# Second attention: the scores by head on 32 rows instead of against masked queries, and the turning of rows as a step of its own

## The chip, the cores and the metric

The kernel runs on one core of one Trainium2 chip. The metric is the device time of one execution in microseconds. A core has five engines that run their own instruction streams: TensorE (PE, matmuls, with weight loads that overlap them), VectorE (DVE), ScalarE (ACT), GpSimd (POOL) and SyncE (SP, which here issues transfers). They wait for one another through semaphores. Matmuls write PSUM, eight banks of 512 f32 columns on 128 partitions; DVE and ACT read results from there.

## The reference

The input is x, 8 blocks of 512 tokens by 256. Two layers follow, each of the form x + attention(layernorm(x)) + mixture of experts(layernorm(x)). The first attention has 16 heads with a causal softmax. Both mixtures have 8 experts, of which each token uses 2. The change touches the second attention only, a gated linear recurrence over 8 heads of 32:

```python
def step(M, inp):
    q_t, k_t, v_t, f_t, g_t, o_t = inp
    M = M * f_t[..., None, None] + g_t[..., None, None] * scale * (k_t[..., :, None] * v_t[..., None, :])
    y_t = jnp.einsum('bhd,bhde->bhe', q_t, M) * o_t[..., None]
    return (M, y_t)
_, yT = jax.lax.scan(step, M0, (qT, kT, vT, fT, gT, oT))
```

q and k are projected from an RMS-normed x and rotated (rope); f, g and o are sigmoids of three more projections; y goes through Wout and a bias is added.

## The kernel before

The recurrence is computed in chunks. A block of S = 512 tokens is NT = 4 chunks of P = 128. Within a chunk, y is a causally masked product: scores (k against q, per head) times exp of the summed logs of f between the two tokens, times v. Between chunks a state m per head is carried: y gets q, weighted by the decay, against m, and m is decayed and gets k, weighted, against v.

The work on a block has two parts. `prep1` prepares: four steps `s_proj` (matmuls pa and pb at L1282 on PE, rope in four instructions from L1297 on DVE, v copied by ACT at L1307), then `s_gates` (the sigmoids by an Exp and a Ln, L1319 and L1323, on ACT, and products on DVE) and `s_decays` (cumulated sums dec on PE, L1343 to L1352, ew and tot by Exp on ACT, and lfx, a copy on ACT). `main1` computes, in steps per chunk c:

- `s_scores(c)`: ACT makes u, eight copies of a triangle of ones, each scaled by a head's log f (L1402). PE turns q and k of the chunk (four transposes qkT, L1406) and ACT copies them to SBUF (qkTs, L1408). Then for each half hf of four heads: PE adds a large negative mask (bf16, L1412) and the summed logs gt·u (L1419) into a bank d; ACT takes exp (de, L1423); DVE spreads the turned queries of four heads over a block-diagonal tile (qb, L1426), so that one full product of 128 rows by 512 columns gives the scores of four heads (a, L1433); DVE multiplies (am, L1434).
- `s_chunk(c)`: for c > 0, the weighted queries qw are turned (qwT, L1449) and copied by ACT (qwTs, L1451). y is made per half from the state (L1454) and four value products, each on a column group of 32 (L1458), and is copied by ACT (yTs, L1466). For c < 3, pm (L1474) is the chunk's addition to the state, taken over by DVE with tm and m (L1488, L1489). po = y·Wout (L1496) is added to x by DVE (L1499).

The chunk step lags one behind the scores: scores 0, scores 1, chunk 0, scores 2, chunk 1, and so on. `interleave` mixes the steps of `main1` of a block with the `prep1` steps of the next block in proportion; the last block of a part has no successor and runs without. After each step `move` deals some steps of other work, in a number worked out from `n_steps`. A scheduler then orders the instructions of each engine by its own estimate of when they can run, so the order on an engine is not just the order of the code. Each engine runs its stream in that order: an instruction that waits holds up all behind it.

`attention1` runs twice. Part a takes blocks 0 to 3 (about 1040 to 1303 us) and deals out the norm, logits, choice of experts (rt_both L315, rank L322, rt_tot L325) and the 128 scatters of rows to the second mixture (L437, on POOL). The experts of the second mixture follow (1303 to 1828 us), among them `prep1` of block 4. Part b takes blocks 4 to 7 (1828 to 1997 us) and deals out the additions of the experts' results (L476, DVE).

PSUM pools of a part: mm (two banks: pa, pb, po and dealt work), tr (two: qkT, qwT), da (two: d and a), y (one), sm (one: dec and pm).

Of the kernel before, what the change touches and what calls it, by code (L numbers as in the profile page):

```python
# [8 lines left out]
F32 = mybir.dt.float32  # L9
# [8 lines left out]
P = 128  # L18
# [66 lines left out]
def tile_two_layers(  # L85
# [1165 lines left out]
    def prep1(b, ap, ps_mm, ps_sm, held1, places=None):  # L1251

        wide = {"tag": "mm", "n": S} if places else {"tag": "sm", "n": 256}
# [86 lines left out]
        def s_decays():  # L1340
            flat = lf.rearrange("p t h -> p (t h)")
            ps = ps_sm.tile([P, wide["n"]], F32, tag=wide["tag"], name=f"dec{b}")
# [27 lines left out]
    def attention1(blocks, part, also, done, held1):  # L1370
        with tc.tile_pool(name=f"a1{part}", bufs=2) as ap, tc.tile_pool(
            name=f"a1mm{part}", bufs=2, space=PSUM
        ) as ps_mm, tc.tile_pool(name=f"a1tr{part}", bufs=2, space=PSUM) as ps_tr, tc.tile_pool(
            name=f"a1da{part}", bufs=2, space=PSUM
        ) as ps_da, tc.tile_pool(name=f"a1y{part}", bufs=1, space=PSUM) as ps_y, tc.tile_pool(
            name=f"a1sm{part}", bufs=1, space=PSUM
        ) as ps_sm:
            wout = second["wout"]
            moves = deque(also(ap, ps_mm))
            n_steps = len(blocks) * (3 * NT + 2)  # L1380
# [8 lines left out]
            def main1(b):  # L1389
# [8 lines left out]
                def s_scores(c):  # L1398

                    u = ap.tile([P, H1, P], F32, tag="u", name=f"u{b}_{c}")  # L1400
                    for h in range(H1):
                        nc.scalar.activation(u[:, h, :], inc, AF.Copy, scale=lf[:, c, h : h + 1])  # L1402
# [6 lines left out]
                    am = ap.tile([P, 2, 4, P], F32, tag="am", name=f"am{b}_{c}")  # L1409
                    for hf in range(2):  # L1410
                        pd = ps_da.tile([P, 4, P], F32, tag="da", name=f"d{b}_{c}_{hf}")
                        nc.tensor.matmul(  # L1412
                            pd,
                            ident_h,
                            mask_gt.unsqueeze(1).to_broadcast([P, 4, P]),
# [3 lines left out]
                        nc.tensor.matmul(  # L1419
                            pd, gt, u[:, 4 * hf : 4 * hf + 4, :], start=False, stop=True  # L1420
                        )
                        de = ap.tile([P, 4, P], F32, tag="de", name=f"de{b}_{c}_{hf}")
                        nc.scalar.activation(de, pd, AF.Exp)  # L1423

                        qb = ap.tile([P, 4, P], F32, tag="qb", name=f"qb{b}_{c}_{hf}")
                        nc.vector.tensor_tensor(  # L1426
                            qb,
                            qkT[:, hf, :].unsqueeze(1).to_broadcast([P, 4, P]),
# [8 lines left out]
                def s_chunk(c):  # L1437
# [3 lines left out]
                    if c:  # L1441
                        pt = ps_tr.tile([P, 4, P], F32, tag="tr", name=f"qwT{b}_{c}")
# [248 lines left out]
```

## Time and profile before

| | us |
|---|---|
| time, median of 3 runs | 2000.53 (1999.66 to 2000.71) |
| the profiled execution | 1999.08 |
| its span (2.1 us lie around it) | 1997.0 |
| mean granted clock of TensorE | 0.96 |
| busy: PE | 1817.4 |
| busy: DVE | 829.4 |
| busy: ACT | 794.5 |
| part a, PE busy of 1040 to 1303 us | 199.9 |
| part b, PE busy of 1828 to 1997 us | 155.7 |

The page of the profile gives busy times per engine, the span in 40 slices, the chain of work that ended last, and groups of instructions. A group's line gives the source line, the engine, the operation, output <- inputs, the shape and the number of instructions; behind the first bar the busy time and the mean in ns of one; behind the second bar the idle time of the engine just before these instructions, and what ended it. Matmuls are pipelined: the length shown of one is more than what it costs, so costs are read from start to start in the timeline. f32 products appear as two instructions each.

### The profile page before, as it was taken

Reading aid. Unit: us, or ns where it says so; the run is one execution under the profiler, and the core shown is the slowest. Engines: PE = TensorE matmul, PEld = TensorE weight load, DVE = VectorE, ACT = ScalarE, POOL = GpSimd, SP = SyncE. Lnnn points to the kernel's source line nnn. Section 1 sums busy time; section 2 is a strip of 40 time slices with the busy share of each in tenths; the row PEclk is TensorE's granted clock in tenths of the full one; section 3 lists DMA queues with packets and bytes.
Section 4 is the critical chain, followed back from the end, with each engine's and each line's share of the span. In section 5 each row is a group of like instructions: output and inputs, shape, how many; then the busy total and the mean of one; then the engine's idle time right before and its main releaser. Section 6 shows DMA issues by size and latency. Waiting matters only on the chain. (4 is left out here: it accounts for less than half of the span.)

```text
span 1997.0 us, 28227 instructions
## 1 busy us (share of the span) xinstructions
PE 1817.4 (91%) x10680; PEld 1241.0 (62%) x10680; DVE 829.4 (42%) x1886; ACT 794.5 (40%) x1452; POOL 401.8 (20%) x457
## 2 busy tenths in 40 slices
PE   5988989999999999998778479999999999999998
PEld 3435655666666665664344235578888889887555
DVE  5453234344344444344676346641111111114865
ACT  2333434444434444444335044533333233325455
POOL 2015531221211221211130661011111111011000
PEclk9999999999999999999789679999999999999899
DMA  8723321754534443332330330076676867581500
GB/s 249 180 93 102 97 65 41 224 191 134 173 122 133 136 172 125 114 120 72 120 111 32 117 106 14 1 258 224 226 256 212 311 216 263 212 301 66 172 11 22
DMA packets 163687, 289.17 MB, mean 145 GB/s; under 512 B 63952, under 2 KB 134624, under 8 KB 152928
## 3 DMA queue, kind: packets, MB, share of 16 engines
q1 hardware_dynamic: 148432, 248.77, 38.3%
q0 software_dynamic: 13088, 36.07, 4.9%
q10 hardware_dynamic: 2032, 2.54, 0.4%
q8 instruction: 84, 1.38, 0.3%
q14 instruction: 51, 0.42, 0.1%
HBM read 206.78 MB, written 67.94 MB: 138 GB/s over the span
## 5 line engine op out<-in xcount | busy, mean ns | idle before, releaser
L659 PE MATMUL gup<-xgT,ew 128*128 128x256 f32 (+1 forms) x2080 | 386.0, 338 | 4.5 <-issue 2.7
L692 PE MATMUL gdn<-ew,hgT 128*128 128x256 f32 x1640 | 376.6, 383 | 0.0
L659 PEld LDWEIGHTS gup<-xgT,ew 128*128 128x128 f32 x2080 | 331.7, 192 | 47.4 <-issue 10.3
L692 PEld LDWEIGHTS gdn<-ew,hgT 128*128 128x128 f32 x1640 | 307.8, 191 | 50.8 <-issue 11.5
L966 DVE TENSOR_REDUCE mx<-m 128x4 f32<-128x2048 f32 (+3 forms) x128 | 190.2, 1486 | 269.5 <-PE m L965 248.7
L991 ACT ACTIVATE pt<-s 128x2048 f32<-128x2048 f32 (+3 forms) x128 | 158.4, 1237 | 199.6 <-PE s L987 186.6
L719 POOL DMA_INDIRECT zd<-yo,row x144 | 140.6, 976 | 466.3 <-DVE yo L710 403.4
L993 POOL TENSOR_SCALAR_AFFINE_SELECT pt<-pt 128x512 f32<-128x512 f32 x128 | 83.8, 655 | 668.2 <-ACT pt L991 666.9
L670 ACT ACTIVATE hgT<-gup,ew 128x256 f32<-128x256 f32 (+1 forms) x376 | 133.9, 423 | 208.4 <-issue 123.6
L710 DVE SCALAR_TENSOR_TENSOR yo<-ew,way,yo 128x256 f32<-128x256 f32 x72 | 31.7, 481 | 300.3 <-ACT yo L708 300.3
L961 PE MATMUL m<-k,q 32*128 32x512 f32 (+3 forms) x1024 | 123.3, 489 | 23.6 <-ACT pt L991 18.4
L987 PE MATMUL s<-qsh,k 32*128 32x512 f32 (+3 forms) x1024 | 113.1, 499 | 31.5 <-DVE mx L966 30.5
L437 POOL DMA_INDIRECT xd<-xr,pos x128 | 126.2, 986 | 55.8 <-issue 44.5
L991 ACT ACT_TABLE_LOAD x52 | 66.7, 1283 | 121.8 <-PE s L987 121.0
L961 PEld LDWEIGHTS m<-k,q 32*128 32x128 f32 x1024 | 48.3, 186 | 80.8 <-ACT pt L991 52.4
L987 PEld LDWEIGHTS s<-qsh,k 32*128 32x128 f32 x1024 | 42.9, 191 | 88.7 <-DVE mx L966 67.9
L1011 PE MATMUL av<-pt,vaug 128*32 128x256 f32 (+3 forms) x1024 | 89.1, 453 | 4.6 <-POOL pt L993 4.5
L1020 DVE STREAM_TRANSPOSE ou<-av 128x512 f32<-128x512 f32 x32 | 22.9, 716 | 146.7 <-PE av L1011 132.5
L708 ACT ACTIVATE yo<-gdn,way 128x256 f32<-128x256 f32 x72 | 30.2, 473 | 125.8 <-PE gdn L692 125.7
L1419 PE MATMUL d<-u,cs 128*128 128x512 f32 x128 | 71.5, 642 | 4.2 <-ACT u L1402 3.9
L1433 PE MATMUL a<-qb,qkTs 128*128 128x512 f32 x128 | 70.0, 629 | 3.8 <-DVE qb L1426 1.9
L1402 ACT ACTIVATE u<-cs,lf 128x128 f32<-128x128 f32 x224 | 72.2, 393 | 0.0
(254 smaller groups left out, 2361.4 us busy)
## 6 DMA issues: line engine op xcount, KB each, us to landing
ew<-in_dram SPq DMA_DIRECT2D x47, 2180.0 KB
ew<-in_dram SPq DMA_DIRECT2D x36, 1024.0 KB
xd<-zero SPq DMA_DIRECT2D x12, 1572.0 KB
z<-zd SPq DMA_DIRECT2D x32, 512.0 KB
xnT<-in_dram SPq DMA_DIRECT2D x22, 512.0 KB
xg<-xd SPq DMA_DIRECT2D x36, 262.0 KB
xg<-xd SPq DMA_DIRECT2D x144, 64.0 KB
xn_d<-l_xn SPq DMA_DIRECT2D x16, 512.0 KB
```

Of the source, the lines that this page charges most:

```text
L437: i = nc.gpsimd.indirect_dma_start(out=self.xd, out_offset=bass.IndirectOffsetOnAxis(ap=self.pos[k][:, at : at + 1], axis=0), in_=held[b][ ...
L659: nc.tensor.matmul(ps[:, j, at : at + m], wu[u][:, k, f * P : (f + 1) * P], x, start=(k == 0), stop=(k == KD - 1),)
L670: nc.scalar.activation(ht[:, f, at : at + m], ps[:, j, at : at + m], AF.Gelu, bias=w[u][2][:, f : f + 1],)
L692: nc.tensor.matmul(ps[:, t, :], ht[:, f, t * P : (t + 1) * P], wd[:, f, :], start=(f == 0), stop=(f == nf - 1),)
L719: d = nc.gpsimd.indirect_dma_start(out=self.r.zd, out_offset=bass.IndirectOffsetOnAxis(ap=row[:, s : s + 1], axis=0), in_=y[:, s, :], in_o ...
L961: nc.tensor.matmul(ps[:, h, :w], q[r, j * P : w], k[r, :w], start=True, stop=False)
L966: last["dve"] = nc.vector.tensor_reduce(mxs[n % 2][:, j, :, HD0], ps[:, :, :w], AX.X, ALU.max)
L987: nc.tensor.matmul(ps[:, h, :w], k[r, i * P : (i + 1) * P], q[r, i * P :], start=True, stop=True)
L991: nc.scalar.activation(e, ps[:, :, :w], AF.Exp, scale=0.25)
L993: last["pool"] = nc.gpsimd.affine_select(out=e[:, :, :P], in_=e[:, :, :P], pattern=[[0, 4], [1, P]], base=0, channel_multiplier=-1, compar ...
L1011: nc.tensor.matmul(ps[32 * h : 32 * h + 32, i * P :], vaugs[b % 2][:, i, c : c + 32], e[:, h, :], start=(i == 0), stop=(i == NT - 1),)
L1402: nc.scalar.activation(u[:, h, :], inc, AF.Copy, scale=lf[:, c, h : h + 1])
```

## The change

The turning of rows and u become a step `s_turn(c)`. `s_scores(c)` takes one tile of four banks. In each bank r lie the scores of heads r and r + 4 in the first two quarters, from products of 32 rows by 128 columns on row group r, and the summed logs of the same heads in the last two. All scores are written first; then mask and gt·u for each bank; then one exp and one product am over all eight heads. qb and the full product a are gone. The order of y is state, values of both halves, state. The chunk step lags two behind the scores, and `n_steps` counts four steps per chunk. Pools: tr has one bank instead of two, da one tile of four banks instead of two of one, sm is gone: pm lies in the second half of qwT's tile, dec in mm.

The core of the diff (left out: `prep1` loses its parameter `ps_sm` and takes dec's bank from mm, and its call during the experts follows):

```diff
@@ -1370,14 +1368,12 @@
     def attention1(blocks, part, also, done, held1):
         with tc.tile_pool(name=f"a1{part}", bufs=2) as ap, tc.tile_pool(
             name=f"a1mm{part}", bufs=2, space=PSUM
-        ) as ps_mm, tc.tile_pool(name=f"a1tr{part}", bufs=2, space=PSUM) as ps_tr, tc.tile_pool(
-            name=f"a1da{part}", bufs=2, space=PSUM
-        ) as ps_da, tc.tile_pool(name=f"a1y{part}", bufs=1, space=PSUM) as ps_y, tc.tile_pool(
-            name=f"a1sm{part}", bufs=1, space=PSUM
-        ) as ps_sm:
+        ) as ps_mm, tc.tile_pool(name=f"a1tr{part}", bufs=1, space=PSUM) as ps_tr, tc.tile_pool(
+            name=f"a1da{part}", bufs=1, space=PSUM
+        ) as ps_da, tc.tile_pool(name=f"a1y{part}", bufs=1, space=PSUM) as ps_y:
             wout = second["wout"]
             moves = deque(also(ap, ps_mm))
-            n_steps = len(blocks) * (3 * NT + 2)
+            n_steps = len(blocks) * (4 * NT + 2)
             left = [n_steps]
 
             def move():
@@ -1395,51 +1391,57 @@
                 def per_head(a):
                     return a.unsqueeze(2).to_broadcast([P, H1, HD1])
 
-                def s_scores(c):
-
-                    u = ap.tile([P, H1, P], F32, tag="u", name=f"u{b}_{c}")
+                turns = {}
+
+                def s_turn(c):
+
+
+                    u = ap.tile([P, 4, 2, P], F32, tag="u", name=f"u{b}_{c}")
                     for h in range(H1):
-                        nc.scalar.activation(u[:, h, :], inc, AF.Copy, scale=lf[:, c, h : h + 1])
+                        nc.scalar.activation(
+                            u[:, h % 4, h // 4, :], inc, AF.Copy, scale=lf[:, c, h : h + 1]
+                        )
                     pt = ps_tr.tile([P, 4, P], F32, tag="tr", name=f"qkT{b}_{c}")
                     flat = qk[c].rearrange("p h d -> p (h d)")
                     for i in range(4):
                         nc.tensor.transpose(pt[:, i, :], flat[:, i * P : (i + 1) * P], ident)
                     qkT = ap.tile([P, 4, P], F32, tag="qkT", name=f"qkTs{b}_{c}")
                     nc.scalar.copy(qkT, pt)
-                    am = ap.tile([P, 2, 4, P], F32, tag="am", name=f"am{b}_{c}")
+                    turns[c] = qkT, u
+
+                def s_scores(c):
+                    qkT, u = turns.pop(c)
+                    ps = ps_da.tile([P, 4, 4, P], F32, tag="da", name=f"da{b}_{c}")
                     for hf in range(2):
-                        pd = ps_da.tile([P, 4, P], F32, tag="da", name=f"d{b}_{c}_{hf}")
+                        for r in range(4):
+                            rows = slice(32 * r, 32 * r + 32)
+                            nc.tensor.matmul(
+                                ps[:, r, hf, :],
+                                qkT[rows, 2 + hf, :],
+                                qkT[rows, hf, :],
+                                start=True,
+                                stop=True,
+                            )
+                    for r in range(4):
                         nc.tensor.matmul(
-                            pd,
+                            ps[:, r, 2:, :],
                             ident_h,
-                            mask_gt.unsqueeze(1).to_broadcast([P, 4, P]),
+                            mask_gt.unsqueeze(1).to_broadcast([P, 2, P]),
                             start=True,
                             stop=False,
                         )
-                        nc.tensor.matmul(
-                            pd, gt, u[:, 4 * hf : 4 * hf + 4, :], start=False, stop=True
-                        )
-                        de = ap.tile([P, 4, P], F32, tag="de", name=f"de{b}_{c}_{hf}")
-                        nc.scalar.activation(de, pd, AF.Exp)
-
-                        qb = ap.tile([P, 4, P], F32, tag="qb", name=f"qb{b}_{c}_{hf}")
-                        nc.vector.tensor_tensor(
-                            qb,
-                            qkT[:, hf, :].unsqueeze(1).to_broadcast([P, 4, P]),
-                            blk.unsqueeze(2).to_broadcast([P, 4, P]),
-                            ALU.mult,
-                        )
-                        pa = ps_da.tile([P, 4, P], F32, tag="da", name=f"a{b}_{c}_{hf}")
-                        nc.tensor.matmul(pa, qkT[:, 2 + hf, :], qb, start=True, stop=True)
-                        nc.vector.tensor_mul(am[:, hf], pa, de)
+                        nc.tensor.matmul(ps[:, r, 2:, :], gt, u[:, r], start=False, stop=True)
+                    de = ap.tile([P, 4, 2, P], F32, tag="de", name=f"de{b}_{c}")
+                    nc.scalar.activation(de, ps[:, :, 2:, :], AF.Exp)
+                    am = ap.tile([P, 4, 2, P], F32, tag="am", name=f"am{b}_{c}")
+                    nc.vector.tensor_mul(am, ps[:, :, :2, :], de)
                     got[c] = am
 
                 def s_chunk(c):
                     am = got.pop(c)
 
                     py = ps_y.tile([P, 2, P], F32, tag="y", name=f"y{b}_{c}")
-                    if c:
-                        pt = ps_tr.tile([P, 4, P], F32, tag="tr", name=f"qwT{b}_{c}")
+                    pt = ps_tr.tile([P, 4, P], F32, tag="tr", name=f"qwT{b}_{c}")
                     if c:
 
                         qw = ap.tile([P, H1, HD1], F32, tag="qw", name=f"qw{b}_{c}")
@@ -1449,19 +1451,23 @@
                             nc.tensor.transpose(pt[:, hf, :], flat[:, hf * P : (hf + 1) * P], ident)
                         qwT = ap.tile([P, 2, P], F32, tag="qwT", name=f"qwTs{b}_{c}")
                         nc.scalar.copy(qwT, pt[:, :2, :])
-                    for hf in range(2):
+                    def of_state(hf):
                         if c:
                             nc.tensor.matmul(
-                                py[:, hf, :], m[:, hf, :], qwT[:, hf, :], start=True, stop=False
+                                py[:, hf, :], m[:, hf, :], qwT[:, hf, :], start=hf == 0, stop=hf == 1
                             )
+
+                    of_state(0)
+                    for hf in range(2):
                         for h in range(4):
                             nc.tensor.matmul(
                                 py[32 * h : 32 * h + 32, hf, :],
                                 v[:, c, 4 * hf + h, :],
-                                am[:, hf, h, :],
-                                start=(c == 0),
-                                stop=True,
+                                am[:, h, hf, :],
+                                start=(c == 0 or hf == 1),
+                                stop=(c == 0 or hf == 0),
                             )
+                    of_state(1)
                     yT = ap.tile([P, KD, P], F32, tag="yT", name=f"yTs{b}_{c}")
                     nc.scalar.copy(yT, py)
 
@@ -1469,7 +1475,7 @@
 
                         kw = ap.tile([P, H1, HD1], F32, tag="kw", name=f"kw{b}_{c}")
                         nc.vector.tensor_tensor(kw, qk[c][:, H1:], per_head(ew[:, 1, c]), ALU.mult)
-                        pm = ps_sm.tile([P, 256], F32, tag="sm", name=f"pm{b}_{c}")
+                        pm = pt[:, 2:, :].rearrange("p i t -> p (i t)")
                         for hf in range(2):
                             nc.tensor.matmul(
                                 pm[:, hf * P : (hf + 1) * P],
@@ -1500,14 +1506,16 @@
 
                 steps = []
                 for c in range(NT):
+                    steps.append(lambda c=c: s_turn(c))
+                    if c > 1:
+                        steps.append(lambda c=c: s_chunk(c - 2))
                     steps.append(lambda c=c: s_scores(c))
-                    if c:
-                        steps.append(lambda c=c: s_chunk(c - 1))
+                steps.append(lambda: s_chunk(NT - 2))
                 steps.append(lambda: s_chunk(NT - 1))
                 return steps
 
             def prep(b):
-                return prep1(b, ap, ps_mm, ps_sm, held1)
+                return prep1(b, ap, ps_mm, held1)
 
             if blocks[0] not in held1:
                 interleave(prep(blocks[0]), [], move)
```

More of the change, by code (lines that the diff above doesn't have):

```diff
@@ L1246, in tile_two_layers, with prep1 @@
         move(len(moves))
-    def prep1(b, ap, ps_mm, ps_sm, held1, places=None):
-        wide = {"tag": "mm", "n": S} if places else {"tag": "sm", "n": 256}
+    def prep1(b, ap, ps_mm, held1, places=None):
         wcat = second["wcat"]
@@ L1341, in s_decays @@
             flat = lf.rearrange("p t h -> p (t h)")
-            ps = ps_sm.tile([P, wide["n"]], F32, tag=wide["tag"], name=f"dec{b}")
+            ps = ps_mm.tile([P, S], F32, tag="mm", name=f"dec{b}")
             nc.tensor.matmul(ps[:, 0:32], inc, flat, start=True, stop=True)
@@ L1588, in tile_two_layers @@
             [lambda b=b: add_bout(b) for b in range(B)],
-            prep1(B // 2, None, ps_p, ps_p, ready, places_of_prep()),
+            prep1(B // 2, None, ps_p, ready, places_of_prep()),
         )
```

## The prediction

> **What bounds the kernel now.** I read the page's busy shares and slices first, then its chain, then the groups by shape, then the stretches of the second attention in the timeline, engine by engine.
>
> ```profile
> span 1997.0 us, 28227 instructions
> PE 1817.4 (91%) x10680; PEld 1241.0 (62%) x10680; DVE 829.4 (42%) x1886; ACT 794.5 (40%) x1452; POOL 401.8 (20%) x457
> ...
> PE   5988989999999999998778479999999999999998
> ...
> PEclk9999999999999999999789679999999999999899
> ...
> PE 38%; issue 3%; DVE 2%; ACT 2%; another core or an unknown queue 2%; DMA 1%; POOL 0%; POOLq 0%; ACTq 0%; SPq 0%; DVEq 0%
> ```
>
> PE is the bound; the other engines are below half. The second attention runs at 1040–1303 us (part a, slices 21 to 26, where the scatters of the second MoE go out and PE falls to 4 tenths) and at 1828–1997 us (part b). Groups by shape:
>
> ```profile
> L1419 PE MATMUL d<-u,cs 128*128 128x512 f32 x128 | 71.5, 642 | 4.2 <-ACT u L1402 3.9 <-issue 0.4
> L1433 PE MATMUL a<-qb,qkTs 128*128 128x512 f32 x128 | 70.0, 629 | 3.8 <-DVE qb L1426 1.9 <-DVE am L1434 1.2 <-ACT de L1423 0.7
> L1426 DVE TENSOR_TENSOR qb<-qkTs,cs 128x512 f32<-128x512 f32 x64 | 42.4, 684 | 18.0 <-ACT qkTs L1408 17.8 <-issue 0.2
> L1423 ACT ACTIVATE de<-d 128x512 f32<-128x512 f32 x64 | 38.2, 597 | 79.8 <-PE d L1419 61.6 <-issue 13.0 <-PE dec L1352 3.9
> ...
> L991 ACT ACTIVATE pt<-s 128x1024 f32<-128x1024 f32 x32 | 32.8, 1024 | 51.7 <-PE s L987 51.6
> ```
>
> The idle times of `a` and `d` are small: PE rarely waits here. In the timeline of PE (start, length, instruction; in brackets the idle time ahead and its releaser) the start-to-start distances give true costs:
>
> ```profile
> 1908.07 1.02 PE L1419 MATMUL d<-u,cs 128*128 128x512 f32 x2
> 1908.93 1.03 PE L1433 MATMUL a<-qb,qkTs 128*128 128x512 f32 x2
> 1909.80 0.38 PE L1449 MATMUL qwT<-cs,qw 128*128 128x128 f32 x2
> ...
> 1912.71 0.58 PE L1454 MATMUL y<-qwTs,m 128*128 128x128 f32 x2 [1.86 <-ACT qwTs L1451]
> 1913.21 0.66 PE L1458 MATMUL y<-am,v 128*32 128x128 f32 x8
> ```
>
> `a` costs 1909.80 − 1908.93 = 0.86 us per half chunk. The last two lines matter as much: PE waited 1.86 us for the copy qwTs, and after it eight value instructions took 0.59 us start to start against 0.36 in the next block (1919.39 to 1919.75): half speed until about 1916.8. ACT's timeline shows why qwTs was late:
>
> ```profile
> 1909.69 1.28 ACT L1423 ACT_TABLE_LOAD   x1
> 1910.99 0.60 ACT L1423 ACTIVATE de<-d 128x512 f32<-128x512 f32 x1
> ...
> 1912.29 0.36 ACT L1451 COPY qwTs<-qwT 128x256 f32<-128x256 f32 x1
> ```
>
> **The scores on PE.** Removed: 64 `a` × 0.857 = 54.9 us. Added: 256 products over 32 rows by 128, f32. The first attention has the shape:
>
> ```profile
> 332.10 0.50 PE L961 MATMUL m<-k,q 32*128 32x128 f32 x8
> 332.53 0.40 PE L965 MATMUL m<-mask_lt,ident_h 128*128 128x128 bf16 x4
> ```
>
> Eight instructions (four products) take 332.53 − 332.10 = 0.43 us, between full-array work on both sides. A chunk has sixteen: 0.43 for the first four with what comes between, 0.21 for the rest, 0.65 against 1.71, so −1.06 × 32 = −34 us. Here a rule speaks against the change: the Trainium skill, "TensorEngine Tiling (Array Packing)", Key Properties, says that a change of tiling mode drains the array. The row has a switch in and one out, and four products one after another would be 4 × 0.214 = 0.857 (a quarter of N=512); so the drain is in the 0.43, worth at most 0.2 of it. The built order splits the sixteen into 1 and 7 or 3, 1 and 4 in some chunks, with po or pa between; at 0.1 to 0.2 per extra switch a block with a successor keeps −3.5 of −4.2. By the row I take −3.5; by a dear drain (0.4 each) it would be −2.
>
> Mask and decay products run as four pairs of 256 columns instead of two of 512: 4 × (0.108 + 0.429) = 2.15 against 2.146, nothing; four weight loads more lie under PE.
>
> **Order of y.** State, values, values, state: two switches fewer for each of 24 chunks. The state product costs 0.42 after value products and 0.32 otherwise, sixteen value instructions 0.57 against 2 × 0.36: −0.2 each, −4.8 us. PE's work falls by 38 to 39 us; a block with a successor from 40.4 (my sum of start-to-start costs) to 36.3.
>
> **DVE.** 64 qb, 42.4 us, go; 64 am of 0.685 become 32. A product of 1024 columns in SBUF takes 1.22 (L1338), one of 512 with a bank read 0.06 to 0.08 more than its issue step of 0.60: 1.28 for 1024. **ACT.** 64 exps of 0.597 become 32 of 1.02, by the first attention's row of that size. No row reads halves of four banks in one instruction; between 0.93 (twice 0.597 less the fixed part) and 1.19 I stay at 1.02. Both engines have spare time, so this is worth nothing where PE is full. Where DVE carries the routing they count: rt_both ends at 1086.8, rank starts at 1087.1, the first of 128 scatters leaves at 1099.4. With six to eight qb of 0.6 gone ahead of it I take the scatters 6 us earlier (0 to 8), of which 4 reach the end (0 to 6), because PE is idle for 46 of the 106 us until 1206 (60.4 busy), mostly not for the routing's sake.
>
> **What is moved: the waits.** The scores' banks are now one tile of four, the turns' one of one, pm lies in qwT's tile. The chain per chunk is PE's end 0.20, exp 1.02, am 1.28, two hops of 0.03 to 0.05: 2.58 us until the next scores may write. In a block with a successor qkT, pa and pb lie under it (0.44 + 1.72 + 0.94 = 3.1): nothing. In blocks 3 and 7, which have none, only 0.9 to 1.9 is there. I laid out the built order of each engine by hand with these durations. Per block with a successor:
> - y of chunk 2 waits for qwTs. On ACT that stands behind the table load (1.28, which itself waits for the last gt·u, because the Ln of the gates is ahead of it), the exp (0.93 to 1.02) and its own 0.37: 0.2 + 1.28 + 0.93 + 0.37 + 0.05 less 0.22 of qwT under it = 2.6 us. Before, the same wait was 1.86. Queued behind it on PE: y, pm, po, the decays, and on ACT yTs.
> - qwT of chunk 1 waits until qkTs has read the only turning bank: 0.2 + 0.58 + 0.05 = 0.84. Before, two banks.
> - y of chunk 3 waits for qwTs: 0.7. The po and other y: 1.1 in all.
>
> Sum 5.2 against 0.8 to 1.9 (mean 1.5) before: +3.7. The routing's moves are dealt over 18 steps per block instead of 14, in the same proportion of the block: no cost.
>
> **The clock.** The granted clock in the slices is 0.7 to 0.9 where PE pauses. The 1.86 us pause cost 1.6 us afterwards (d 1.46 long against 1.02, and y), one at 1861 3.2 us; a pause of 0.80 at 1957 cost nothing. The Trainium skill, "TensorE: Matmul & The Clock Gate", Part 1, puts the loss behind an idle window of about 3.4 us; by it 2.6 us would cost nothing, by the rows about 2 per block. I go by the rows: 2.1 against 1.2 before, +0.9.
>
> Net per block with a successor −4.1 + 3.7 + 0.9 = +0.5, six of them +3. Blocks 3 and 7: the last decays at 1960.5 to PE's end at 1992.5 are 32.0; by hand 31.2 of work and 3.8 of waits, 35.0, and 1 for the clock, +4 each, +8. Routing −4. Part b's start: the first qkTs now stands behind eight u of 0.305 (1830.9 against d at 1829.2), made up by chunk 1: 0. Sum +7 on the profiled 1999.1 (span 1997.0 and 2.1 around it; median 2000.5, 1.4 above). I round down, since a hand layout finds waits more easily than it finds overlap: 2006.
>
> **The rivals.**
> - *The removed work counts.* Place: ACT, between the last gt·u and qwTs of chunk 2, and chain da–exp–am in blocks 3 and 7. If these waits fall under PE work, −39 gives 1961; with half of them 1980. Decision point: the wait ahead of y of chunk 2; below about 2.0 us the clock stays up and each block gains, above it loses. For it: PE 91%, few idle times in the groups. Against: the single banks. Faster; chance 0.32, mostly at 1978 to 1995.
> - *Gain and waits cancel.* 1997 to 2004; 0.17.
> - *The send stretch.* Between 1112.7 and 1144.4 the chain has 31.72 us of "another core or an unknown queue": DVE, ACT and PE stand while scatters run, and nothing in the trace names why. It may be 15 longer or shorter whatever the change intends; above 2014 if longer. For it: the stall began and ended at instructions of this attention (tm on DVE, yTs on ACT), which the change shifts. Against: the scatters, their 1.27 us each and their queue stay as they are. Chance 0.12 above 2014, as much below in the first rival.
> - *Four do not run at once*: sixteen in a row, 1.71 per chunk, no gain: +34, about 2030. Against: the 0.43 row. 0.05.
> - The forecast itself, 2004 to 2014: 0.34.
>
> A difference of 0.2% (4 us) is about what a measurement of this kernel tells from none. So faster 0.32, same 0.17, slower 0.51. Range 1980 to 2022: below lies the full gain, above the serial scores. The slower case alone is 2004 to 2014.
>
> **What would show it.** Scores of sixteen at 0.65; no qb on DVE; a pause of 2.0 to 3.0 us ahead of y of chunk 2 by ACT qwTs in each block with a successor, and y or d after it at half speed; block to block 43 as before; last decays to end about 36. Wrong if that pause is under 1 us, if blocks take under 41, or if the stretch 1100 to 1206 changes by more than 6.

## The result, and the profile after

The changed kernel takes 2012.18 us (median of 4 runs, 2008.76 to 2015.62) against 2000.1 for the kernel before (1996.95 to 2000.71): ratio 1.0072, 95% interval 1.0051 to 1.0093. Run a second time, beside another set of runs of the kernel before, the ratio is 1.0093 (1.0066 to 1.0119). It is slower by 0.7 to 0.9%; forecast were 2006 us and a range of 1980 to 2022.

The page of the changed kernel first: span, PE's busy time, the slices of PE and its clock, and the chain by engine.

```profile
span 2010.8 us, 29220 instructions
...
PE 1790.3 (89%) x11256; PEld 1261.3 (63%) x11256; DVE 782.4 (39%) x1790; ACT 789.3 (39%) x1420; POOL 400.4 (20%) x457
...
PE   5888989999999999998777358899999999999897
...
PEclk9998999999999999999789669899999999999999
...
PE 35%; another core or an unknown queue 3%; DVE 3%; issue 2%; ACT 2%; DMA 1%; POOL 0%; ACTq 0%; POOLq 0%; DVEq 0%; SPq 0%
```

PE's busy time fell by 27 us (1817.4 to 1790.3) and the span grew by 13.8. The groups by shape show where it went: the scores (L1418, 512 instructions) are cheap, but the state product of y, L1454 before with 3.7 us of idle time ahead of it (all by ACT qwTs), is L1456 now and waits 39.2. The first line is the kernel before, the others are the changed kernel.

```profile
L1454 PE MATMUL y<-qwTs,m 128*128 128x128 f32 x96 | 23.3, 327 | 3.7 <-ACT qwTs L1451 3.7
```

```profile
L1418 PE MATMUL da<-qkTs 32*128 32x128 f32 x512 | 34.1, 324 | 1.0 <-ACT qkTs L1409 0.7
L1435 ACT ACTIVATE de<-da 128x1024 f32<-128x1024 f32 x32 | 32.8, 1024 | 81.1 <-PE da L1433 61.4 <-remote 12.3 <-PE pb L1280 4.9
L1456 PE MATMUL y<-qwTs,m 128*128 128x128 f32 x96 | 27.3, 372 | 39.2 <-ACT qwTs L1453 39.1
L1437 DVE TENSOR_TENSOR am<-da,de 128x1024 f32<-128x1024 f32 x32 | 39.2, 1224 | 91.5 <-ACT de L1435 91.5
```

The durations that the forecast had to take from other rows are as it took them: exp 1.02, am 1.22 (1.28 taken). Now block 6 on PE (start, length; in brackets the idle time ahead and its releaser), first the scores of chunk 1, which stand together, then the tail of the block:

```profile
1940.19 0.73 PE L1418 MATMUL da<-qkTs 32*128 32x128 f32 x16
1940.85 0.28 PE L1426 MATMUL da<-mask_gt,ident_h 128*128 128x256 bf16 x1
...
1954.41 0.60 PE L1407 MATMUL qkT<-cs,qk 128*128 128x128 f32 x4
1955.74 0.44 PE L1451 MATMUL qwT<-cs,qw 128*128 128x128 f32 x2 [0.73 <-ACT qkTs L1409]
1956.11 0.50 PE L1418 MATMUL da<-qkTs 32*128 32x128 f32 x6
1956.64 0.49 PE L1456 MATMUL y<-qwTs,m 128*128 128x128 f32 x2
...
1958.49 0.48 PE L1418 MATMUL da<-qkTs 32*128 32x128 f32 x2
1958.91 1.13 PE L1502 MATMUL po<-wout,yTs 128*128 128x256 f32 x4
1959.97 0.50 PE L1418 MATMUL da<-qkTs 32*128 32x128 f32 x8
1960.40 0.28 PE L1426 MATMUL da<-mask_gt,ident_h 128*128 128x256 bf16 x1
...
1965.47 0.55 PE L1456 MATMUL y<-qwTs,m 128*128 128x128 f32 x2 [2.50 <-ACT qwTs L1453]
1965.94 1.08 PE L1463 MATMUL y<-am,v 128*32 128x128 f32 x16
1966.95 0.80 PE L1456 MATMUL y<-qwTs,m 128*128 128x128 f32 x2
```

The scores of chunk 3 stand in three pieces of 6, 2 and 8 instructions: 0.53, 0.42 and 0.43 us from start to start, 1.38 together, where the sixteen of chunk 1 in a row take 0.66. Then PE stands for 2.50 us, and the value products behind it take 1.01 from start to start, where they take 0.57 at full clock. ACT in the same stretch shows what the pause is made of:

```profile
1962.83 1.28 ACT L1435 ACT_TABLE_LOAD   x1 [1.16 <-PE da L1433]
1964.13 1.02 ACT L1435 ACTIVATE de<-da 128x1024 f32<-128x1024 f32 x1
1965.05 0.37 ACT L1453 COPY qwTs<-qwT 128x256 f32<-128x256 f32 x1
```

Table load, exponential of all eight heads, copy: this is the wait that the forecast put at 2.6 us. To see the sums, take two stretches of part b, from the decays of block 6 to those of block 7 and from there to the end. The columns are the stretch, its length, busy time (and instructions) of PE, weight loads, DVE, ACT and POOL, the granted clock, DMA share and GB/s. Before:

```profile
1917.68:1960.46 42.78, 41.98 (x223) 24.84 (x221) 30.11 (x66) 23.24 (x62) 0.00 (x0) 1.00 0.04 13
1960.46:1992.30 31.84, 30.91 (x188) 17.82 (x187) 16.53 (x36) 16.69 (x46) 0.00 (x0) 1.00 0.05 17
```

After:

```profile
1924.89:1969.65 44.76, 40.98 (x283) 28.50 (x282) 24.09 (x54) 23.52 (x58) 0.00 (x0) 0.92 0.04 13
1969.65:2006.03 36.38, 30.19 (x277) 21.56 (x275) 11.51 (x26) 14.19 (x35) 0.00 (x0) 1.00 0.05 16
```

In the block with a successor the idle time grew from 0.80 to 3.78 and the clock fell from 1.00 to 0.92, so that even the smaller work is 41 us long. The 0.92 is a mean: the clock stands at 0.50 in two stretches of 3.4 us and at 1.00 between them.

```profile
1928.22:1931.63 3.41, 3.41 (x11) 2.85 (x12) 0.23 (x1) 0.96 (x2) 0.00 (x0) 0.50 0.00 0
1931.63:1965.76 34.13, 30.87 (x214) 20.30 (x212) 20.28 (x44) 19.53 (x46) 0.00 (x0) 1.00 0.05 16
1965.76:1969.18 3.42, 3.42 (x26) 2.71 (x26) 1.12 (x4) 2.37 (x8) 0.00 (x0) 0.50 0.02 5
```

The second follows the pause of this block at once; the first comes 6 us after the like pause of block 5, which ended at 1921.98. In the last block the idle time grew from 0.9 to 6.2. The lengths of the block and of the last stretch came out equal, within 0.01 us, in the second profile of either kernel.

From the last wo (output) product of the first attention to PE's end by stages, in us; the first column of each pair is the profile of the first comparison, the second that of the second one. "Decays" are the first dec matmuls of a block's preparation, so the third are those of block 2, made while block 1 runs; "experts" ends where the last run of expert matmuls, 9.7 us long, begins.

| stage | before | after |
|---|---|---|
| last wo of the first attention to third decays (scatters within) | 192.2, 188.0 | 192.5, 192.1 |
| third to fourth decays | 42.8, 42.9 | 43.5, 43.2 |
| fourth decays to first expert matmul | 47.0, 47.0 | 54.5, 50.4 |
| experts | 495.9, 495.5 | 494.1, 494.1 |
| experts to decays of block 6 | 104.5, 108.5 | 100.0, 104.8 |
| decays of block 6 to 7 | 42.8, 42.8 | 44.8, 44.8 |
| from there to PE's end | 31.8, 31.8 | 36.4, 36.4 |
| sum | 957.0, 956.5 | 965.8, 965.8 |

So the second attention and what lies around it explain 9 us of the loss in both pairs. The medians differ by 12 to 15; the profiles do not show where the rest is, since single profiles differ by several us ahead of the second attention already, where the code is the same (the last wo starts at 1034 to 1040 us).

### The profile page after: what moved, and what is told of

Same layout as the page of the kernel before. It is cut to its first block, busy times and chain, and to the rows that moved or that the text cites. A ratio compares the mean times of both kernels' runs of the same rounds, so it can differ in the third digit from the quotient of the medians.

```text
span 2010.8 us, 29220 instructions
## 1 busy us (share of the span) xinstructions
PE 1790.3 (89%) x11256; PEld 1261.3 (63%) x11256; DVE 782.4 (39%) x1790; ACT 789.3 (39%) x1420; POOL 400.4 (20%) x457
## 5 line engine op out<-in xcount | busy, mean ns | idle before, releaser
L437 POOL DMA_INDIRECT xd<-xr,pos x128 | 126.1, 985 | 58.5 <-issue 46.0
L987 PEld LDWEIGHTS s<-qsh,k 32*128 32x128 f32 x1024 | 42.9, 191 | 91.1 <-DVE mx L966 69.5
L1437 DVE TENSOR_TENSOR am<-da,de 128x1024 f32<-128x1024 f32 x32 | 39.2, 1224 | 91.5 <-ACT de L1435 91.5
L1433 PE MATMUL da<-u,cs 128*128 128x256 f32 x256 | 74.5, 393 | 0.0
```

Source lines behind the costliest of these rows:

```text
L437: i = nc.gpsimd.indirect_dma_start(out=self.xd, out_offset=bass.IndirectOffsetOnAxis(ap=self.pos[k][:, at : at + 1], axis=0), in_=held[b][ ...
L987: nc.tensor.matmul(ps[:, h, :w], k[r, i * P : (i + 1) * P], q[r, i * P :], start=True, stop=True)
L1433: nc.tensor.matmul(ps[:, r, 2:, :], gt, u[:, r], start=False, stop=True)
```

## The experiments

The twelve runs fall into three sets, each on another chip (numbered 8, 10 and 0) and each with its own runs of the kernel before, which took 1932.7 us in the first set, 1992.6 in the second and 1993.9 in the third. Only ratios and stages are compared across sets. The changed kernel itself was not run on the chip of the first set, so a ratio of that set against its ratio rests on the ratios carrying over from chip to chip.

**The table load moved away** (first set).

```diff
             nc.scalar.activation(ln, den[:, :, :H1], AF.Ln)
+            if places is None:
+                warm = ap.tile([P, 1], F32, tag="warm", name=f"warm{b}")
+                nc.scalar.activation(warm, ln[:, 0, 0:1], AF.Exp)
```

> The changed kernel with one exponential of a single column right behind the logarithm of the gates, so that ACT changes its table back there and not in front of the exponential of chunk 3. Theory (the gain is eaten by the wait for qwTs of chunk 2, 2.5 to 3.0 us per block with a successor in the changed kernel, and by the low clock after it): the wait falls by the 1.28 of the table load to about 1.2 in six blocks, 8 us, and the half-speed stretches after it go, up to 8 more: 1997 to 2004. Rival (the switches of the array between 32-row and full products are the cost, waits are hidden elsewhere): the pause shrinks and another one takes its place, 2010 to 2014.

Measured: ratio 1.0026 (1.0015 to 1.0037), 0.005 to 0.007 below the changed kernel's two ratios (9 to 13 us). Decays of block 6 to 7 take 42.1 us instead of 44.8, the last stretch 36.0. On PE, in that block:

```profile
1884.55 1.13 PE L1505 MATMUL po<-wout,yTs 128*128 128x256 f32 x4 [1.29 <-ACT yTs L1475]
...
1889.77 0.49 PE L1459 MATMUL y<-qwTs,m 128*128 128x128 f32 x2 [1.16 <-ACT qwTs L1456]
```

The pause at chunk 2 fell from 2.50 to 1.16, as expected, and the slow clock after it is gone (1.00 over the whole block). But 1.29 us of it came back one instruction earlier: po of chunk 1 now waits for yTs, which stands behind both table loads. The rival is refuted for the block; a part of its second half (the next wait takes over) holds.

**PE kept busy in the pause** (first set). Five products that nothing reads, in the six blocks with a successor. Left out of the cut: y's tile becomes a full bank, so that they have a place.

```diff
                         nc.scalar.copy(qwT, pt[:, :2, :])
+                        if c == 2 and b not in (3, 7):
+                            for _ in range(5):
+                                nc.tensor.matmul(
+                                    py[:, 2:, :].rearrange("p i t -> p (i t)"),
+                                    ident,
+                                    cs[:, C_ID : C_ID + 2 * P],
+                                    start=True,
+                                    stop=True,
+                                )
```

> The changed kernel with five products that nothing reads (2.15 us of 256 columns) on PE in the pause ahead of y of chunk 2, in the six blocks with a successor. Theory (the pause costs twice, once itself and once by the clock after it): the time of the pause stays, the half-speed rows behind it (po 1.73 instead of 0.97, qkT 0.85 instead of 0.44) go, 1.5 to 3 us in four or five places: 2002 to 2007. Rival (a pause of 2.5 us is too short to lower the clock and the slow rows have another cause): 2011 to 2014.

Measured: ratio 1.0017 (1.0006 to 1.0029). PE in the same place of block 6, and the two stretches of the table above:

```profile
1881.25 2.33 PE L1456 MATMUL y<-cs 128*128 128x256 f32 x10
1883.91 0.49 PE L1465 MATMUL y<-qwTs,m 128*128 128x128 f32 x2 [0.34 <-ACT qwTs L1453]
1884.33 0.64 PE L1472 MATMUL y<-am,v 128*32 128x128 f32 x16
...
1886.50 1.13 PE L1511 MATMUL po<-wout,yTs 128*128 128x256 f32 x4 [0.67 <-ACT yTs L1481]
```

```profile
1844.69:1887.47 42.78, 40.42 (x293) 27.95 (x292) 24.02 (x53) 23.38 (x58) 0.00 (x0) 1.00 0.04 13
1887.47:1923.85 36.38, 30.19 (x277) 21.59 (x275) 11.44 (x25) 14.18 (x35) 0.00 (x0) 1.00 0.05 16
```

The wait for qwTs is as long as it was (2.33 of useless work and 0.34 idle), the value products behind it take 0.57 instead of 1.01, and the block is 42.8 instead of 44.8 at clock 1.00 instead of 0.92. The last block, which got no such products, is unchanged. So these pauses are what lowers the clock. In this block that is worth 2.0 us net, 2.7 without the 0.67 that po newly waits, because two slow stretches fell into it: 1.3 us for one stretch, about half of the pause. In part a's block from the third decays to the fourth, which held one, the gain is 0.4 to 0.7 net (42.78 against 43.47 and 43.20).

**The scores alone undone** (first set). Queries spread on DVE and full products, eight of 128 columns, in the new structure.

```diff
+                        qb = ap.tile([P, 4, P], F32, tag="qb", name=f"qb{b}_{c}_{hf}")
+                        nc.vector.tensor_tensor(
+                            qb,
+                            qkT[:, hf, :].unsqueeze(1).to_broadcast([P, 4, P]),
+                            blk.unsqueeze(2).to_broadcast([P, 4, P]),
+                            ALU.mult,
+                        )
                         for r in range(4):
-                            rows = slice(32 * r, 32 * r + 32)
                             nc.tensor.matmul(
                                 ps[:, r, hf, :],
-                                qkT[rows, 2 + hf, :],
-                                qkT[rows, hf, :],
+                                qkT[:, 2 + hf, :],
+                                qb[:, r, :],
```

> The changed kernel with the scores made as before by full products (spread queries on DVE, eight products of 128 columns, 1.71 us per chunk instead of 0.65), the rest of the change kept. Theory (the 32-row scores are a true gain on PE of 1.06 us per chunk, and the new order and banks are the loss): +25 to +34, so 2037 to 2046, and the structure alone then costs about 40 against the kernel before. Rival (PE work saved here lies under waits anyway): less than +10, 2012 to 2022.

Measured: ratio 1.0234 (1.0202 to 1.0266), that is 0.014 to 0.016 above the changed kernel's two ratios, 28 to 32 us. Decays to decays take 49.4 (+4.6, where four times 1.06 are 4.2), the last stretch 43.9 (+7.5). The chips differ, but the stages agree: from the third decays to PE's end, without the scatters' stretch, this run takes 803.0 us and the changed kernel 773.3 and 773.8 in its two profiles. So the scores on 32 rows are a true gain of about 30 us, nearly all that they save. What comes with them, the banks, the one exponential and the order of the steps, is this run's own loss against the kernel before: 2.0 to 2.7%, 39 to 51 us. Scores on 32 rows in the structure of before were not tried.

**The order of y alone** (first set): the kernel before with state, eight value products, state.

```diff
-                    for hf in range(2):
-                        if c:
...
+                    of_state(0)
+                    for hf in range(2):
...
+                    of_state(1)
```

> The kernel before with nothing but the new order of y: state, eight value products, state. By the rows of before this is -0.2 us for each of 24 chunks: 1995.3 (-4.8). Rival: the state product of the second half was hidden or the switch is not what the 0.1 is: no change, 2000.

Measured: ratio 0.9975 (0.9962 to 0.9987), −4.8 us of 1932.7. The expected −4.8 to the digit is luck within an interval of ±2.4, but the sign is clear: this part of the change is a gain by itself. It was measured alone on one chip only.

**The changed kernel again** (second set).

> The changed kernel itself, beside the kernel before on the same chip, so that the other runs can be set against it. In the last call the kernel before took 1932.7 us against 2000 at first, and in all of its four profiles the 94 us between the first two sets of decays (before) had become 42 to 54. Theory (the loss lies in waits and clock of every block, not in the stretch where the scatters go out): the ratio stays at 1.005 to 1.010, and the blocks by themselves are as in the first profile of the changed kernel: 44.8 between two decays of part b, 36.4 at the end. Rival (the ratio came from the scatter stretch and from the 5 us by which the first attention began later): 0.985 to 1.000.

Measured: ratio 1.0093 (1.0066 to 1.0119), blocks as in the table above. The rival is refuted.

**The kernel before again** (second set).

> The kernel before, for its profile on the same chip. All theories: ratio 1.000 within 0.002; the stretch from the first to the second decays near 45 us instead of 94, blocks of 42.8 as before, 31.8 from the last decays to the end.

Measured: ratio 0.9994 (0.9973 to 1.0014). The blocks came out as expected, but the stretch of the scatters did not: it took 96.6 us here, as in the first profile. It is short only in the first set.

**Exponential and am in halves** (second set), in two tiles of two banks.

```diff
-                    ps = ps_da.tile([P, 4, 4, P], F32, tag="da", name=f"da{b}_{c}")
+                    pss = [
+                        ps_da.tile([P, 2, 4, P], F32, tag="da", name=f"da{b}_{c}_{g}")
+                        for g in range(2)
+                    ]
...
+                        if r % 2:
+                            g = slice(r - 1, r + 1)
+                            nc.scalar.activation(de[:, g], pss[r // 2][:, :, 2:, :], AF.Exp)
+                            nc.vector.tensor_mul(am[:, g], pss[r // 2][:, :, :2, :], de[:, g])
```

> The changed kernel with exponential and am in two halves of two banks each, in two tiles, so that the first half starts 1.1 us before the last gt-u ends and the next scores may enter the first tile earlier. Theory (the chain exp 1.02, am 1.28 is uncovered in the blocks without a successor and sets the pause at y of chunk 2): last blocks -2 each (36.4 to 34.5), pause at chunk 2 from 2.5 to about 2.1, in all -5 to -8 against the changed kernel. Rival (more instructions on ACT and DVE, 64 of 0.60 and 0.68 instead of 32 of 1.02 and 1.28, cost as much as they free): 0 to +4.

Measured: ratio 1.0032 (1.0015 to 1.0048), 0.006 below the changed kernel in the same set (12 us, more than expected; 9 between the medians). The last stretch is 34.3, as expected. The block is 41.8 instead of 44.8, more than expected: the table load waits for the first half only, the pause is 1.47 instead of 2.50, and the clock stays at 1.00 behind it. In part a's block of the same kind the clock is 0.96 and the block 43.1: a slow stretch came some 6 us after the same pause of 1.47 in the block ahead of it. The rival is refuted.

**Halves and the early exponential** (second set).

> Both: the exponential of one column behind the logarithm, and halves in two tiles. Theory: pauses at chunk 2 fall to 0.8, blocks to 41.5, last blocks to 34.5: 8 to 14 below the changed kernel and 2 to 8 below the kernel before. Rival (each wait that goes is replaced by the next on ACT: yTs behind two table loads, 1.3 us in the run with the early exponential): level with the kernel before within 0.2%.

Measured: ratio 1.0055 (1.0037 to 1.0072), above the kernel before, and not below the halves alone. The rival was right in kind, and even too mild: the pause at chunk 2 is 0.73, but po of chunk 1 waits 1.68 us for yTs behind two table loads, its products are slow after that (1.44 long instead of 1.13), and the block is 43.6. In part a's block the same two waits were followed by no slow stretch, and it is 42.1. Two waits of one cause, moved but not removed.

**The chunk step one behind the scores** (third set).

```diff
                     steps.append(lambda c=c: s_turn(c))
-                    if c > 1:
-                        steps.append(lambda c=c: s_chunk(c - 2))
                     steps.append(lambda c=c: s_scores(c))
-                steps.append(lambda: s_chunk(NT - 2))
+                    if c:
+                        steps.append(lambda c=c: s_chunk(c - 1))
```

> The changed kernel with the chunk step one behind the scores, as before, instead of two. In the built order the sixteen score instructions then stand together in every chunk, not in pieces of 2 and 14 or 6, 2 and 8 with full products between them. Theory (each piece costs 0.35 to 0.4 us of switching, three extra pieces per block with a successor; the wait at chunk 2 by the table load and the one exponential stays as it is): blocks from 44.8 to about 43.7, last blocks unchanged, in all -3 to -8 against the changed kernel. Rival (the lag of two is what hides exponential and am of a chunk, without it y waits for am): +3 to +10.

Measured: ratio 1.0129 (1.0085 to 1.0172), not separable from the changed kernel's; the block is 45.8 instead of 44.8. My expectation missed. The pieces are gone, sixteen score instructions in 0.66 in every chunk, but the pause at chunk 2 grew:

```profile
1966.82 0.80 PE L1456 MATMUL y<-qwTs,m 128*128 128x128 f32 x2 [4.32 <-ACT qwTs L1453]
```

```profile
1961.73 2.44 ACT L1401 ACTIVATE u<-cs,lf 128x128 f32<-128x128 f32 x8
1964.19 1.28 ACT L1435 ACT_TABLE_LOAD   x1
1965.48 1.02 ACT L1435 ACTIVATE de<-da 128x1024 f32<-128x1024 f32 x1
1966.40 0.37 ACT L1453 COPY qwTs<-qwT 128x256 f32<-128x256 f32 x1
```

The eight u of the next block, which ACT had finished before the last gt·u in the changed kernel, now stand ahead of the table load as well. The clock of this block is 0.96, that of part a's like block 0.89. The rival's reason (y waiting for am) is not what happened either: the releaser is again ACT qwTs. The last stretch fell to 34.7.

**A bank for qkT alone** (third set), qwT and pm in the free half of y's bank.

```diff
-                    py = ps_y.tile([P, 2, P], F32, tag="y", name=f"y{b}_{c}")
-                    pt = ps_tr.tile([P, 4, P], F32, tag="tr", name=f"qwT{b}_{c}")
+                    py = ps_y.tile([P, 4, P], F32, tag="y", name=f"y{b}_{c}")
...
-                            nc.tensor.transpose(pt[:, hf, :], flat[:, hf * P : (hf + 1) * P], ident)
+                            nc.tensor.transpose(py[:, 2 + hf, :], flat[:, hf * P : (hf + 1) * P], ident)
...
-                        pm = pt[:, 2:, :].rearrange("p i t -> p (i t)")
+                        pm = py[:, 2:, :].rearrange("p i t -> p (i t)")
```

> The changed kernel with qwT and pm in the unused half of y's bank, so that the turning bank holds qkT alone. Theory (the single turning bank costs 0.73 us per block with a successor and 1.15 twice per last block by the wait for qkTs): these waits go, blocks -0.7, last blocks -1 to -2, in all -4 to -8 against the changed kernel. Rival (qwT now waits for yTs and tm of the chunk before instead, in one bank with y): 0 to +4.

Measured: ratio 1.0063 (1.0047 to 1.0078), 0.001 to 0.003 below the changed kernel's, but the intervals overlap. The block is 41.6, a good deal less than expected: the turning of rows for the next block moved into the pause and splits it into 0.63 and 1.57, and the clock stays at 1.00 up to the next decays. The last stretch, 36.7, did not gain, against the expectation: its idle time fell by only 0.6 (36.66 − 31.06 = 5.6 us), and its clock is 0.95 where it was 1.00.

**Halves and a bank for qkT** (third set).

> Halves in two tiles and qwT with pm in y's bank, without the early exponential, whose second table load stood ahead of yTs of chunk 1. Theory: the savings add up, blocks 41 (41.8 with halves alone), last blocks 33.5, level with the kernel before or up to 6 below it. Rival: as halves alone, 5 above the kernel before.

Measured: ratio 0.9988 (0.9972 to 1.0005), level with the kernel before. In the blocks it is well below it; the pause ahead of y of chunk 2 is 1.04:

```profile
1908.89 0.49 PE L1460 MATMUL y<-qwTs,m 128*128 128x128 f32 x2 [1.04 <-ACT qwTs L1457]
```

```profile
1912.30:1952.80 40.50, 38.48 (x283) 26.66 (x282) 24.95 (x58) 23.91 (x62) 0.00 (x0) 1.00 0.04 14
1952.80:1986.77 33.97, 30.50 (x267) 22.08 (x265) 12.36 (x31) 14.22 (x39) 0.00 (x0) 1.00 0.05 16
```

Both blocks of this kind that I could compare are 40.5 (42.8 before), and part b from the end of "experts" in the table of stages is 172.0 against 179.2 and 183.2. Part a from the last wo to the first expert matmul is 280.9 against 282.0 and 277.9: there nothing is gained, since the stretch from the last wo to the third decays, in which the scatters run, is 192.4. It is 188 to 195 in every kernel of the second and third set.

**The kernel before with the order of y and the early exponential** (third set).

> The kernel before with the new order of y, which by itself measured 0.9975, and the exponential of one column behind the logarithm. Theory (the wait of 1.86 us for qwTs behind the table load, and the 1.6 us of clock after it, are there before the change too, in some blocks): 0.2 to 0.4% below the order of y alone, ratio 0.993 to 0.996. Rival (the second table load stands ahead of yTs and takes it back): 0.997 to 0.999.

Measured: ratio 0.999 (0.9971 to 1.0008), not below the order of y alone (0.9975). The rival was right: po of the block of 43.3 us waits 2.28 for yTs (1.13 with the order of y alone).

The only version whose interval lies below the kernel before is the order of y alone.

## Why the prediction was right, and where its steps were off

The range held the time and the side was right, by the cause that was forecast: work leaves PE, and waits on ACT and a slower clock take its place. The forecast had +7 us on the profiled run; the stages sum to +9. The terms of the blocks came out nearly as forecast in sum; the term of the routing did not. Here is PE from the third decays to its end, without the experts: blocks 2 to 7, the first and the second pair of profiles, in us. In the column of the forecast the four blocks with a successor count at its terms, and blocks 3 and 7 at +4 each (2.9 of waits over the 0.9 of before, and 1 of clock).

| blocks 2 to 7 | before | after | change | forecast |
|---|---|---|---|---|
| length | 259.5, 263.6 | 269.6, 270.1 | +10.1, +6.5 | +10 |
| PE idle | 15.7, 16.6 | 38.8, 36.5 | +23.1, +19.9 | +20.6 |
| stretches at clock 0.50 | 13.7, 20.8 | 27.3, 34.1 | +13.6, +13.3 | |
| loss by them, at 1.3 us for each 3.4 | 5, 8 | 10, 13 | +5, +5 | +5.6 |

What is left is PE's work, some 18 us less where the forecast had 16.4. Step by step, with the block from the decays of 6 to those of 7:

- **Scores.** Sixteen in a row take 0.66 (0.65 forecast). The rule on the drain of the array (the Trainium skill, "TensorEngine Tiling (Array Packing)", Key Properties) was given too little room: a piece that is cut off costs 0.36 to 0.4 ((1.38 − 0.66)/2 and 1.06 − 0.66), not 0.1 to 0.2, so a block's scores take 3.76 and not 3.3. The work of a block fell from 42.0 to 38.3 (PE's busy time at clock 1.00, in the runs with the early exponential and with halves), −3.7 where −4.1 was forecast.
- **Waits.** The three that were named are there: 2.50 at y of chunk 2 (2.6), 0.73 at qwT of chunk 1 (0.84), 0.52 at y of chunk 3 (0.7). The many small ones are not: 3.8 in all (5.2). Before 0.8 (1.5): +3.0 where +3.7 was forecast.
- **Clock.** In this block the term is most off: +2.7 (busy 40.98 at clock 0.92 against 38.3), where the block before had none and the forecast took +0.9 (2.1 against 1.2). Two slow stretches fell into it; in sum over the blocks the term fits, as the table shows. Going by the rows and not by the rule of one idle window was right: the run with PE kept busy shows that pauses of 2.5 us lower the clock.
- **Net of a block** −3.7 + 3.0 + 2.7 = +2.0, as measured, forecast +0.5. But not six times. The fourth decays come only 0.3 to 0.7 later, at a clock of 0.96 and 0.97. Blocks 4 and 5 together became 4.5 and 3.7 us shorter: some 10 us of work went, and their idle time grew by 8.0 in the first pair and 4.7 in the second. Before, block 4 had a pause of 1.90 us by DVE qb, with slow clock behind it, and that qb is gone. But this does not explain the gain: the changed kernel has slow stretches there too, and in the second pair more of them than the kernel before.
- **Last blocks.** Part b +4.5 (+4). Part a +7.5 in the first profile and +3.4 in the second: with idle times of the same kind, and in the first profile 4 us more by a clock of 0.91 (0.99 in the second).
- **Routing.** Forecast −4, measured +0.3 and +4.1 up to the third decays. Here the step failed. The scatters to the second mixture are 64, not 128 (the 128 of L437's group are those of both mixtures), and the first of them did leave earlier, 59.4 us behind the start of the last wo instead of 64.2 (−4.8, forecast −6). The last one starts some 3.5 us earlier, and the stretch from the first to the last, about the 1100 to 1206 of the forecast, is 104.0 and 103.8 instead of 102.6 and 102.7, so it did not change by more than the 6 that the forecast named as a sign of being wrong. But the end of the stretch is not set by when the first scatter leaves. In it engines stand still for reasons that the profile does not name, before at tm on DVE and after at ew on ACT, in both profiles of each kernel. DVE of the kernel before, then ACT of the changed one, both in the second set ("remote" is another core or an unknown queue):

```profile
1145.23 0.49 DVE L1488 TENSOR_TENSOR tm<-pm,cs 128x128 f32<-128x128 f32 x2 [31.76 <-remote]
```

```profile
1180.03 0.22 ACT L1357 ACTIVATE ew<-dec 128x64 f32<-128x64 f32 x1 [19.98 <-remote]
```

So PE's gain in blocks 0 and 1 does not show in those runs. It does not show in the first set either, where these standstills are missing: up to the third decays the runs with the early exponential and with PE kept busy take 134.0 us, the kernel before with the order of y 131.4. What the standstills are and what sets this stretch stays open; a cause was not tried.
- **Experts** took 1.4 to 1.8 less in these profiles, but not because of the change: all runs lie at 493.5 to 494.2 or at 495.5 to 495.9, the kernel before with the order of y at 494.1, the changed one with halves and a bank for qkT at 495.7.

That the sum came within 2 us of the stages is in part luck. The routing and blocks 0 and 1, −3 together in the forecast, came out at +0.3 and +4.1; the experts' −1.4 to −1.8 and, in the second pair, 3.5 us less for blocks 2 to 7 made up for a part of that. And no term of it stands for the 3 to 6 us by which the medians differ more than the stages.

Of the rivals, "the removed work counts" was decided where it said, at the pause ahead of y of chunk 2: with the pause at 1.04 us (halves and own bank) the block falls to 40.5. "Four do not run at once" is refuted by 0.66 for sixteen. "The send stretch" moved by 0.3 and 4.1, not by 15.

## What to carry to other kernels

A saving on the bounding engine is only as good as the chain behind the instructions that it moves together: merging two exponentials into one and all heads into one tile put 1.28 + 1.02 + 0.37 us of ACT work in series with PE, and a pause of 2.5 us cost on average half its length once more through the clock. Look for the place where an engine changes its table between two waits of the bounding one, and for tiles that are released as a whole; splitting both in halves, with a bank that holds the turned q and k alone, brought back what the change had lost. Measure the parts of a change one by one: here the order of y was a gain by itself, the scores on 32 rows were a gain of 30 us, and the structure built around them lost more than that.

## What was not expected of the hardware

- Behind some pauses of PE the granted clock falls to 0.50, for 3.41 us or a multiple of it. It can fall at once (value products in 1.01 instead of 0.57 at 1965.94) or some 6 us later (po in 1.73 instead of 1.06 from 1929.4 on, after the pause that ended at 1921.98). The two profiles of the changed kernel have eight pauses of 2.50 us ahead of y of chunk 2, in blocks 1, 2, 5 and 6, and eight such stretches behind them: two behind some, none behind others.
- The length of a pause does not decide it. Two profiles of the changed kernel have the same pause at the same instruction, and only in the second did the clock fall. The first, then the second, each with the instruction behind the pause and the row of a stretch there (third from the end: the granted clock):

```profile
1841.38 1.96 PE L1280 MATMUL pa<-wcat,xnT 128*128 128x512 f32 x4 [3.76 <-DVE rb L1301]
1841.38:1877.00 35.62, 29.84 (x229) 20.11 (x230) 29.38 (x52) 22.89 (x54) 0.00 (x0) 1.00 0.50 167
```

```profile
1830.42 3.38 PE L1280 MATMUL pa<-wcat,xnT 128*128 128x512 f32 x4 [3.75 <-DVE rb L1301]
1829.89:1833.31 3.42, 2.89 (x4) 1.17 (x4) 3.37 (x8) 3.42 (x13) 0.00 (x0) 0.50 0.94 307
```

A pause of 1.47 was followed by a slow stretch in one block and by none in another. The two stretches of block 6 start eleven times 3.41 us apart, as if on a fixed grid; if so, it matters where on it a pause falls. That was not tested.
- The kernel before took 1933 us on one chip and 1993 to 2000 in the other sets. On that chip the stretch from the first to the third decays was 94.3 us long (in the kernel with the order of y alone), against 150.8 in the second set for the kernel before, with the long standstills missing. Whether the chip is the reason was not tested.
